# Two decoder layers on one core: the mask of layer 1's context attention added by half-row products

## The chip, the cores and the metric

The kernel runs on one core of one Trainium2 chip. A core has a matrix engine (TensorE, PE in the profile, with its weight loads shown apart as PEld), a vector engine (VectorE, DVE), an activation engine (ScalarE, ACT), a general engine (GpSimd, POOL) and a synchronisation engine (SyncE, SP), which here does nothing but issue transfers (DMAs). Each engine takes its instructions in program order. The metric is the device time of one execution in microseconds (us), the median of several runs.

## The reference

Two post-norm decoder layers work on x of shape 32 x 128 x 128 (batch, tokens, width) with a context of the same shape. In order: a recurrent mix (RWKV), a block with self attention, attention to the context and a feed-forward part (16 heads of 64), a mixture of 8 experts, then in layer 1 a self attention with rotary positions (16 heads of 8), the attention to the context that is changed here, and a mixture of experts with a capacity. A layer norm of the sum follows each. The part that is changed:

```
def _L1_xattn_ref(query, key, value, mask, Wq, bq, Wk, bk, Wv, bv, Wo):
    HEADS = 16
    HEAD_DIM = 8
    SCALE = HEAD_DIM ** (-0.5)
    NEG_INF = -1000000000.0
    ...
    scores = jnp.einsum('bhqd,bhkd->bhqk', q, k) * SCALE
    scores = jnp.where(mask == 0, NEG_INF, scores)
    attn = jax.nn.silu(scores)
    out = jnp.einsum('bhqk,bhkd->bhqd', attn, v)
    out = out.transpose(0, 2, 1, 3).reshape(B, Sq, HIDDEN)
    return out @ Wo.T
...
x = _layernorm(x + _L1_xattn_ref(x, ctx_1024, ctx_1024, mask_Bx1xSxS2_ik1, ...), axis=-1)
```

The mask is an integer array of 32 x 1 x 128 x 128 and is the same for all heads. The attention has a SiLU in place of a softmax, so no maximum and no sum over the row is needed.

## The kernel before

**Tiling.** The batch of 32 is cut into 8 groups of 4 (`G = 4`, so 512 columns a group). Each layer part turns a group into 8 units, and each unit into steps with a lag counted in units (the tables `L5` to `L8`). `build` places all steps of all parts on one time axis, sorts them and writes them out in that order, so that groups and parts follow one another in a software pipeline. A scheduler then orders each engine's instructions; within what data and buffers allow it can move them against the order in which they were written. Buffers come from pools with a tag and a number of buffers (`TAG`, `BUFS`, for PSUM `BANK`, `BANKS`) that are handed out in turn, so that a new use of a buffer waits for the last reader of its old content.

**Layer 1's attention to the context** is `xat_units`. For a group:

- `load` brings x and the context; `pre` transposes x (`xT_ps`, L228) and splits both into a rounded part and its remainder (`split`, L147 and L148).
- `one` projects to queries and keys with three products (`mm3`, L154 to L156) and ACT adds a bias (L1081).
- `part` cuts queries and keys into three bf16 parts on POOL (`parts3`, L783 to L786), and `spill` writes these to DRAM (L807, L809, L810).
- `take` reads them back as a stack (`stack`, L821): head by head, 64 rows for each parity of the head, with the parts of q and k arranged so that one product of 64 rows gives an exact score. Layer 1's self attention goes the same way.
- `mload` loads the group's mask as integers (L1066, tile `mi`, tag `xb`, 2 buffers) and `mask` turns it on DVE into 0 or -1e9 in bf16 (L1070, tile `m`, tag `msk`, 2 buffers).
- `probs(j)`, eight units a group, each with one batch entry and eight heads: two products of the identity with the mask (L1104) start two PSUM banks of 512 columns, one for each parity, the mask being read four times over by a stride of zero. Then eight products of 64 rows and 128 columns (L166, from `block`) add the scores of four heads to each bank. ACT takes the tanh (L1116) and DVE combines it to the SiLU (L1117).
- `values(j)` multiplies with the values in array tiles of 24 columns (L166, `PV<-e`), ACT copies (L853), `oproj` projects (L1130) and adds the residual (L1136), and a layer norm follows (L238, L240, L254). The result is stored (L223) and loaded by the next part (L214).

The order on PE: `block` ties its products to one another in the order in which they are given, and to the block before. The mask products L1104 are issued outside of `block`, so the scheduler can put them apart from the eight products that follow them. Products of three shapes meet in this stage: 128 rows by 128 columns of the array (printed `128*128`), half rows (`64*128`) and the values' `128*24`.

The order on SP: nearly all transfers of the stage go through its queue: x, context, mask, spill and stack of this part and of the self attention before it, and the loads of the expert layer after it. An issue that has to wait for a buffer or for data holds all issues behind it.

Of the kernel before, what the change touches and what calls it, by code (L numbers as in the profile page):

```python
# [11 lines left out]
BF = mybir.dt.bfloat16  # L12
U8 = mybir.dt.uint8
I32 = mybir.dt.int32
AF = mybir.ActivationFunctionType
ALU = mybir.AluOpType
# [6 lines left out]
G = 4  # L23
# [26 lines left out]
L6 = dict(pre=0, rope=2, v=3, part=5, spill=12, take=16, smax=19, mrow=19, mread=4, probs=29, values=30,  # L50
          norm=32, oproj=34, done=38)
L7 = dict(pre=1, one=2, v=3, part=4, spill=9, mask=13, take=13, probs=14, values=16, oproj=18, ln=22, done=24)
L8 = dict(pre=3, logit=4, route=8, load=7, start=11)
FC = dict(load=-11, pre=-10, fc1=-8, fc2=-7, post=-6, done=-5)

# [5 lines left out]
class Later:  # L61


    def __init__(self, get):
        self.get = get
# [5 lines left out]
class Net:  # L71
    def __init__(self, ctx, tc, a, ngroups):
        self.ctx, self.tc, self.nc, self.a, self.ng = ctx, tc, tc.nc, a, ngroups
        nc = self.nc
        self.cst = ctx.enter_context(tc.tile_pool(name="cst", bufs=1))
        self.wp = ctx.enter_context(tc.tile_pool(name="wp", bufs=1))
        self.ps = ctx.enter_context(tc.tile_pool(name="ps", bufs=1, space=PSUM))
        self.sm = ctx.enter_context(tc.tile_pool(name="sm", bufs=3))
        self.dp = ctx.enter_context(tc.tile_pool(name="dp", bufs=1, space=bass.MemoryType.DRAM))
        self.hand = {}  # L80
        self.toturn, self.topv = [], []
        self.last = self.seen = self.pvz = self.dst = self.spare = self.spare2 = None
        self.wk = ctx.enter_context(tc.tile_pool(name="wk", bufs=1))
        self.ident = self.cst.tile([128, 128], F32, name="ident")
        make_identity(nc, self.ident)
        self.identb = self.cst.tile([128, 128], BF, name="identb")
        nc.gpsimd.tensor_copy(self.identb, self.ident)
        self.mhalf = self.cst.tile([128, G], F32, name="mhalf")
        nc.gpsimd.memset(self.mhalf, -0.5)
        self.rev = self.cst.tile([128, 8], F32, name="rev")  # L90
        nc.gpsimd.iota(self.rev, [[-1, 8]], base=8, channel_multiplier=0,
                       allow_small_or_imprecise_dtypes=True)
# [961 lines left out]
    def xat_units(self, g, getw, done):  # L1054
        nc = self.nc
        w = Later(getw)
        st = {}
        b3 = lambda t: t.rearrange("p (b s) -> p b s", s=128)

        def load():  # L1060
            st["x"] = self.getx(g)
            st["c"] = self.ctx_load(g)

        def mload():
            st["mi"] = self.t("mi", [G, 128], I32)
            nc.sync.dma_start(out=st["mi"], in_=self.a["mask1"][:, g * G:(g + 1) * G, :])  # L1066

        def mask():
            st["m"] = self.t("m", [G, 128], BF)
            nc.vector.tensor_scalar(st["m"], st.pop("mi"), 0.0, -1e9, ALU.is_equal, ALU.mult)  # L1070

        def pre():
            st["xh"], st["xl"] = self.split(self.xT_ps(st.pop("x")), "cx")
            st["kh"], st["kl"] = self.split(st.pop("c"), "cc")

        def one(i, xh, xl):
            f = slice(i * 128, i * 128 + 128)
            qp = self.pst("one")
            self.mm3(qp, w["w"][0][:, f], w["w"][1][:, f], xh, xl)
            t1 = self.t("xt")  # L1080
            nc.scalar.activation(t1, qp, AF.Identity, bias=w["b"][:, i:i + 1])  # L1081
            st["t", i] = t1

        def part(i):
            if i == 0:
                st["p"] = self.parts()
            self.parts3(st.pop(("t", i)), [st["p"][:, a, i, :] for a in range(3)], self.t("xr"), i == 1)

        def spill():
            st["d"] = self.spill(g + self.ng, st.pop("p"))  # L1090

        def take(h):
            st["s", h] = self.stack(st["d"], h)

        def vproj(b):
            st["v", b] = self.v9proj(g + self.ng, b, st["kh"], st["kl"], w["w"][0][:, 256:384], w["w"][1][:, 256:384],
                                     w["bv"])

        def probs(j):
            b, pq = j // 2, j % 2  # L1100
            t = slice(b % 2 * 128, b % 2 * 128 + 128)
            s = [self.pst("silu1" if j % 2 else "silu0") for _ in range(2)]
            for par in range(2):
                nc.tensor.matmul(out=s[par], lhsT=self.identb,  # L1104
                                 rhs=st["m"][:, b, :].unsqueeze(1).to_broadcast([128, 4, 128]), start=True, stop=False)
            calls = []
            for k in range(4):
                for par in range(2):
                    r = slice(par * 64, par * 64 + 64)
                    calls.append((s[par][:, k * 128:(k + 1) * 128], st["s", b // 2][r, pq * 4 + k, 1, t],  # L1110
                                  st["s", b // 2][r, pq * 4 + k, 0, t], dict(start=False, stop=k == 3)))
            self.block(calls)
            ps = []
            for par in range(2):
                p = self.t("xp")
                nc.scalar.activation(p, s[par], AF.Tanh, scale=0.5 * 8 ** -0.5)  # L1116
                st["last", j] = nc.vector.scalar_tensor_tensor(p, p, 1.0, s[par], ALU.add, ALU.mult)  # L1117
                ps.append(p)
            st["p", j] = ps

        def values(j):
            st["ob", j // 2] = self.values9(j, st["v", j // 2], st.pop(("p", j)), st.get(("ob", j // 2)),
                                              st.pop(("last", j)))

        def oproj(b):
            ob = st.pop(("ob", b))
            if b == 0:
                st["op"] = self.pst("xout").rearrange("p (b d) -> p b d", d=128)
            for s in range(4):
                nc.tensor.matmul(out=st["op"][:, b, :], lhsT=ob[:, s * 128:(s + 1) * 128],  # L1130
                                 rhs=w["wo"][:, s * 128:(s + 1) * 128], start=s == 0, stop=s == 3)
            if b == G - 2:
                st["x"] = self.getx(g)
            if b == G - 1:
                res = self.tok("xres")
                nc.vector.tensor_tensor(res, st["op"], st["x"], ALU.add)  # L1136
                st["ln"] = self.ln(res, 1e-5)

        units = []
        for j in range(8):  # L1140
            u = [(L7["probs"], lambda j=j: probs(j), 2), (L7["values"], lambda j=j: values(j), 1)]
            if j == 0:
                u += [(0, load), (L7["pre"], pre), (L7["spill"], spill), (L7["mask"] - 2, mload), (L7["mask"], mask)]
                u += [(L7["v"] + b, lambda b=b: vproj(b)) for b in range(G)]
                for i in range(2):
                    u += [(L7["one"] + 2 * i, lambda i=i: one(i, *((st["kh"], st["kl"]) if i else (st["xh"], st["xl"])))),
                          (L7["part"] + 2 * i, lambda i=i: part(i))]
            if j % 4 == 0:
                u.append((L7["take"], lambda h=j // 4: take(h)))
            if j % 2:  # L1150
                u.append((L7["oproj"], lambda b=j // 2: oproj(b)))
            if j == 7:
                u += [(L7["ln"], lambda: st.update(y=st["ln"]())), (L7["done"], lambda: done(st["y"]))]
            units.append([p if len(p) > 2 else (*p, -p[0]) for p in u])
        return units
# [341 lines left out]
def prep(i):  # L1497
    c = np.ascontiguousarray
    f = np.float32
    pairs = lambda w: c(w.reshape(8, 128, 128).transpose(1, 0, 2).reshape(128, 1024))  # L1500
    d = {
        "xtok": c(i["x"].transpose(1, 0, 2)),
        "xT": c(i["x"].transpose(2, 0, 1).reshape(128, 4096)),
        "ctxT": c(i["ctx_1024"].transpose(2, 0, 1).reshape(128, 4096)),
        "mask0": c(i["mask_BxS2_bk0"].reshape(4096)),
        "rwkv_w": c(np.concatenate([i["L0_attn_" + n].T for n in ("Wk", "Wv", "Wr", "Wo")], axis=1)),
        "rwkv_v": c(np.stack([i["L0_attn_" + n] for n in
                              ("mix_k", "mix_v", "mix_r", "spatial_decay", "spatial_first")], axis=1)),
    }
# [23 lines left out]
    b = [i["L1_attn_bq"], i["L1_attn_bk"]]  # L1533
# [17 lines left out]
    wo = np.zeros((4, 4, 32, 128), f)  # L1551
    wo[:, :, :8] = i["L1_xattn_Wo"].T[rows].reshape(4, 4, 8, 128)
    d["x1_wo"] = c(wo.reshape(4, 128, 128).transpose(1, 0, 2).reshape(128, 512))
    d["mask1"] = c(i["mask_Bx1xSxS2_ik1"][:, 0].transpose(2, 0, 1))
    d["m1_gate"] = c(i["L1_ffn_gate_w"].T)
    w1, w3, w2 = (i["L1_ffn_" + n] for n in ("w1", "w3", "w2"))

# [23 lines left out]
```

## Time and profile before

| what | value |
|---|---|
| median of 3 runs | 1859.68 us (1859.35 to 1861.64) |
| the profiled execution, own time | 1864.75 us |
| its span | 1863.0 us, 47015 instructions |
| TensorE clock granted, mean | 0.969 |
| PE busy | 1673.1 us, 90% of the span |
| weight loads | 1360.9 us, 73% |
| DVE busy | 1387.5 us, 74% |
| ACT busy | 1183.3 us, 64% |
| POOL busy | 865.5 us, 46% |
| chain that ended last, by engine | PE 56%, DVE 18%, ACT 9%, DMA 6%, POOL 5%, issue 4% |
| mask products L1104 | 128, from 1382.3 to 1612.9 us |
| mask operations L1070 | 8, from 1192.7 to 1546.9 us |
| mask loads L1066 | 8 of 256 KB, from 1189.9 to 1498.2 us |

How to read it: the page describes one execution. A row of a timeline gives start, duration, engine, line, operation, what it writes and reads (`out<-in`), and the shape; `x8` means that eight such instructions that followed one another are put together. PE's instructions are pipelined, so that durations of neighbours overlap and the distance between starts says more about their cost. "PEclk" is the share of full speed that the clock of TensorE was granted. `SPq` is the time in which SP issues a transfer. In a view of waits, "A <- B" means that A stood idle until B was done. Numbers of buffers are left out of the names.

### The profile page before, as it was taken

The page shows a single profiled execution, that of the slowest core. Times are in us where ns is not written, and L with a number is a line of the kernel's source. Part 1 is how long each engine was busy: PE and PEld are TensorE (multiplying, and loading weights), DVE is VectorE, ACT ScalarE, POOL GpSimd, SP SyncE. Part 2 cuts the span into 40 slices and gives each one's busy share as a digit, 9 for nine tenths or more (in the row PEclk, how much of TensorE's full clock was granted, in tenths as well). Part 3 has the DMA queues.
Part 4 walks back from the last instruction along what each step waited for, and adds up shares of the span by engine and source line. Part 5 has one row for each costly group of instructions (what it writes and reads, how often), then busy time and mean ns, then how long its engine had stood idle before and what let it go on. Part 6 is the DMA issues. An engine that isn't in the chain of part 4 may idle for free.

```text
span 1863.0 us, 47015 instructions
## 1 busy us (share of the span) xinstructions
PE 1673.1 (90%) x16682; PEld 1360.9 (73%) x16682; DVE 1387.5 (74%) x5384; ACT 1183.3 (64%) x3833; POOL 865.5 (46%) x1201
## 2 busy tenths in 40 slices
PE   4898889989999999999899999989779888898898
PEld 3677667767778788887788888866556555688898
DVE  7878988877777777776675767777655767689896
ACT  2775767768777777787645454346567555556664
POOL 4545555564454444453334444336333422246455
PEclk7999999999999999999999999999889989899999
DMA  5101011110110000100134435479878987222222
GB/s 159 36 32 37 26 37 39 34 53 26 48 48 26 26 14 20 48 13 16 62 107 145 159 121 129 111 184 203 192 204 214 226 198 190 74 80 94 94 90 70
DMA packets 148779, 171.58 MB, mean 92 GB/s; under 512 B 13128, under 2 KB 100176, under 8 KB 146064
## 3 DMA queue, kind: packets, MB, share of 16 engines
q1 hardware_dynamic: 145808, 154.95, 31.2%
q0 software_dynamic: 1584, 11.54, 1.5%
q8 instruction: 131, 2.15, 0.5%
q10 hardware_dynamic: 1152, 2.10, 0.3%
q14 instruction: 104, 0.85, 0.2%
HBM read 114.81 MB, written 55.31 MB: 91 GB/s over the span
## 4 chain that ended last, share of the span: by engine, by line
PE 56%; DVE 18%; ACT 9%; DMA 6%; POOL 5%; issue 4%; SPq 1%; ACTq 0%; POOLq 0%; DVEq 0%
PE PV L166 7%; PE mm L154 6%; PE mm L532 6%; PE S L749 6%; PE S L166 5%; PE mm L155 5%; PE mm L156 5%; ACT e L474 5%; DMA x<-x 3%; DVE e L469 3%; PE PT L1327 3%; PE PT L165 2%; DVE x L254 1%; POOL e L478 1%; PE S L598 1%
## 5 line engine op out<-in xcount | busy, mean ns | idle before, releaser
L474 ACT ACTIVATE e<-e,nm 128x128 f32<-128x128 f32 x1024 | 397.5, 390 | 95.6 <-POOL nm L471 95.5
L478 POOL TENSOR_TENSOR e<-e,ri 128x512 f32<-128x512 f32 x256 | 267.3, 1048 | 258.8 <-DVE ri L476 192.8
L469 DVE CUSTOM_DVE_ANT_0 e<-S,msk 128x128 f32<-128x128 f32 x1024 | 225.2, 282 | 11.9 <-PE S L166 11.7
L474 ACT ACTIVATION_READ_ACCUMULATOR e<-e,nm 128x1 f32 x1024 | 192.3, 188 | 0.0
L166 PEld LDWEIGHTS S<-qk 64*128 64x128 f32 x2048 | 126.0, 189 | 72.0 <-issue 41.2
L166 PE MATMUL S<-qk 64*128 64x128 f32 x2048 | 150.1, 286 | 29.6 <-DVE pt L492 20.6
L154 PE MATMUL mm<-xs,w 128*128 128x512 f32 x296 | 130.6, 444 | 35.0 <-ACT xs L147 11.5
L166 PE MATMUL PV<-pt,v 128*64 128x128 f32 x2048 | 141.7, 281 | 3.5 <-DVE big L516 2.5
L476 DVE RECIPROCAL ri<-su 128x4 f32<-128x4 f32 x256 | 43.8, 172 | 135.4 <-ACT e L474 134.8
L738 ACT ACTIVATE v<-mm,col_moe_b 128x512 f32<-128x512 f32 x128 | 85.1, 684 | 79.4 <-PE mm L156 78.9
L749 PEld LDWEIGHTS S<-w,v 128*128 128x128 f32 x1024 | 128.6, 191 | 7.8
L749 PE MATMUL S<-w,v 128*128 128x128 f32 x1024 | 133.7, 276 | 0.0
L492 ACT COPY pt<-PT 128x256 f32<-128x256 f32 x256 | 81.6, 371 | 68.6 <-PE PT L165 68.2
L532 PE MATMUL mm<-w,big 128*128 128x128 f32 x1024 | 122.1, 277 | 0.0
L532 PEld LDWEIGHTS mm<-w,big 128*128 128x128 f32 x1024 | 117.5, 192 | 4.9 <-issue 2.9
L155 PE MATMUL mm<-xs,w 128*128 128x512 f32 x296 | 118.6, 401 | 1.6 <-DVE xs L148 1.6
L166 PEld LDWEIGHTS PV<-pt,v 128*64 128x64 f32 x2048 | 110.6, 138 | 12.7 <-DVE big L516 2.9
L156 PE MATMUL mm<-xs,w 128*128 128x512 f32 x296 | 117.8, 398 | 0.0
L166 PE MATMUL PV<-e,w 128*24 128x128 f32 x2048 | 88.1, 292 | 26.5 <-ACT e L974 11.3
L267 POOL TENSOR_SCALAR rsqv<-bmv 128x4 f32<-128x4 f32 (+1 forms) x73 | 14.4, 197 | 202.1 <-DVE bmv L240 185.5
L853 ACT COPY v<-PV 128x256 f32<-128x256 f32 x128 | 47.9, 374 | 92.3 <-PE PV L166 91.8
L154 PEld LDWEIGHTS mm<-xs,w 128*128 128x128 f32 x296 | 55.5, 189 | 61.5 <-ACT xs L147 16.2
(306 smaller groups left out, 4782.2 us busy)
## 6 DMA issues: line engine op xcount, KB each, us to landing
x<-x SPq DMA_DIRECT2D x151, 256.0 KB
big<-d_st SPq DMA_DIRECT2D x52, 512.0 KB
pt<-d_w SPq DMA_DIRECT2D x64, 256.0 KB
d_st<-qk SPq DMA_DIRECT2D x48, 256.0 KB
d_st<-qk SPq DMA_DIRECT2D x16, 768.0 KB
d_w<-big POOLq DMA_DIRECT2D x11, 1024.0 KB, 5.2
w<-d_w SPq DMA_DIRECT2D x7, 1024.0 KB
w<-d_st SPq DMA_DIRECT2D x12, 512.0 KB
```

The lines of the kernel that those rows point to most:

```text
L154: mm(out=out, lhsT=wh, rhs=xh, start=True, stop=False)
L155: mm(out=out, lhsT=wh, rhs=xl, start=False, stop=False)
L156: mm(out=out, lhsT=wl, rhs=xh, start=False, stop=True)
L166: return self.nc.tensor.matmul(out=out, lhsT=lhsT, rhs=rhs, **more)
L469: self.seen = nc.vector.tensor_tensor_reduce(e[:, t], s[h][:, t], msk[:, t], 1.0, NEG, ALU.add, ALU.max, mx[:, b:b + 1])
L474: nc.scalar.activation(e[:, t], e[:, t], AF.Exp, bias=nm[:, b:b + 1], scale=0.125, accum_out=su[:, b:b + 1])
L478: i = nc.gpsimd.tensor_tensor(e3, e3, ri.unsqueeze(2).to_broadcast([128, G, 128]), ALU.mult)
L492: last = (nc.vector.tensor_copy if h else nc.scalar.copy)(d, s_)
L532: nc.tensor.matmul(out=o[:, b, :], lhsT=st["ot", p // 4][:, p % 4, b * 128:(b + 1) * 128], rhs=w["wo"][:, p * 128:(p + 1) * 128], start=p ...
L738: nc.scalar.activation(h, hp, AF.Gelu, bias=w["b1"][:, k:k + 1])
L749: nc.tensor.matmul(out=o[:, b, :], lhsT=hs[i][:, b * 128:(b + 1) * 128], rhs=w["w2"][:, k * 128:k * 128 + 128], start=i == 0, stop=i == 1)
L1327: nc.tensor.matmul(out=o[:, 0:N], lhsT=a_, rhs=b_, start=n == 0, stop=n == len(prods) - 1)
```

## The change

The mask is loaded, converted and multiplied in another arrangement.

- On the host, `mask1` of (128 queries, 32 entries, 128 keys) becomes (128, 32, 2, 128): the 128 queries are cut into two halves, and partition p holds, for both halves, the row p mod 64. So each of the two halves of the partitions has the whole mask.
- A group's mask is therefore twice as large. It is loaded and converted in two steps of two batch entries (`mload(h)`, `mask(h)`), the second one `MSTEP = 2` units after the first.
- A second matrix beside the identity, `rollb`, has the identity's column halves exchanged. It is made once by two copies on POOL.
- In `probs`, the two products of 128 rows become four of 64 rows: for each half z of the queries and each parity a product of 64 rows of `identb` or `rollb` with the mask's half, over the same 512 columns. The two parities use different halves of the array's rows and different PSUM banks. They are the first four calls of the unit's `block`, ahead of its eight products.

```
+MSTEP = 2
...
+        self.rollb = self.cst.tile([128, 128], BF, name="rollb")
+        nc.gpsimd.tensor_copy(self.rollb[:, 0:64], self.ident[:, 64:128])
+        nc.gpsimd.tensor_copy(self.rollb[:, 64:128], self.ident[:, 0:64])
...
-        def mload():
-            st["mi"] = self.t("mi", [G, 128], I32)
-            nc.sync.dma_start(out=st["mi"], in_=self.a["mask1"][:, g * G:(g + 1) * G, :])
-
-        def mask():
-            st["m"] = self.t("m", [G, 128], BF)
-            nc.vector.tensor_scalar(st["m"], st.pop("mi"), 0.0, -1e9, ALU.is_equal, ALU.mult)
+        def mload(h):
+            st["mi", h] = self.t("mi", [2, 2, 128], I32)
+            nc.sync.dma_start(out=st["mi", h], in_=self.a["mask1"][:, g * G + h * 2:g * G + h * 2 + 2])
+
+        def mask(h):
+            if h == 0:
+                st["m"] = self.t("m", [G, 2, 128], BF)
+            nc.vector.tensor_scalar(st["m"][:, h * 2:h * 2 + 2], st.pop(("mi", h)), 0.0, -1e9, ALU.is_equal, ALU.mult)
...
             s = [self.pst("silu1" if j % 2 else "silu0") for _ in range(2)]
-            for par in range(2):
-                nc.tensor.matmul(out=s[par], lhsT=self.identb,
-                                 rhs=st["m"][:, b, :].unsqueeze(1).to_broadcast([128, 4, 128]), start=True, stop=False)
             calls = []
+            for z in range(2):
+                for par in range(2):
+                    r = slice(par * 64, par * 64 + 64)
+                    calls.append((s[par], (self.rollb if z ^ par else self.identb)[r],
+                                  st["m"][r, b, z, :].unsqueeze(1).to_broadcast([64, 4, 128]),
+                                  dict(start=z == 0, stop=False)))
...
-                u += [(0, load), (L7["pre"], pre), (L7["spill"], spill), (L7["mask"] - 2, mload), (L7["mask"], mask)]
+                u += [(0, load), (L7["pre"], pre), (L7["spill"], spill), *((L7["mask"] - 2 + MSTEP * h, lambda h=h: mload(h)) for h in range(2)),
+                      *((L7["mask"] + MSTEP * h, lambda h=h: mask(h)) for h in range(2))]
...
-    d["mask1"] = c(i["mask_Bx1xSxS2_ik1"][:, 0].transpose(2, 0, 1))
+    m = i["mask_Bx1xSxS2_ik1"][:, 0].transpose(2, 0, 1).reshape(2, 64, 32, 128).transpose(1, 2, 0, 3)
+    d["mask1"] = c(np.concatenate([m, m]))
```

In the compiled program PE has 256 mask products where it had 128, each with its own weight load; DVE has 8 operations more, SP 8 transfers more and POOL 2 copies more. Outside of these every engine has the same instructions, in a partly different order from about 1190 us on.

## The prediction

> **What bounds the kernel now.** I read the page's time slices, then the busy time by stretch around the changed lines, then those lines' own rows, then the queues they stand in.
>
> ```profile
> PE   4898889989999999999899999989779888898898
> PEclk7999999999999999999999999999889989899999
> DMA  5101011110110000100134435479878987222222
> ```
>
> TensorE (PE) is at eight tenths or more nearly everywhere, so PE is the bound of the whole. The exception is slices 29 to 35 (1304 to 1630 us), where PE falls to 7 and 8 and its clock to 8, while the DMA engines stand at 7 to 9 until 1584. The changed lines run there. By stretch (PE, weight loads, DVE, ACT, POOL busy; then clock, DMA share, GB/s):
>
> ```profile
> 1382.00:1400.00 18.00, 9.24 (x95) 4.63 (x94) 2.64 (x8) 6.90 (x15) 4.05 (x5) 0.62 1.05 239
> 1400.00:1470.00 70.00, 63.87 (x873) 42.39 (x872) 49.40 (x116) 47.98 (x103) 30.75 (x41) 1.00 0.93 220
> 1470.00:1526.00 56.00, 45.09 (x532) 29.55 (x536) 34.03 (x72) 27.65 (x57) 16.73 (x20) 0.85 0.85 211
> 1526.00:1573.00 47.00, 45.81 (x638) 29.71 (x638) 36.13 (x76) 31.29 (x68) 12.17 (x14) 1.00 0.94 214
> 1573.00:1622.00 49.00, 37.30 (x295) 27.34 (x295) 30.95 (x89) 22.94 (x59) 9.07 (x10) 0.79 0.16 51
> ```
>
> Two stretches (70 and 47 us) have PE 91% and 97% busy at full clock: less PE work shortens them. The others hold PE gaps and a lowered clock: what ends the gaps sets them. The waits of PE between 1180 and 1615 us name it (total, times, longest):
>
> ```profile
> PE PT L228 <- DMA x<-x: 12.9, 4, 5.9
> ```
>
> These are the transposes of x of a later group; three of the four lie at 1472, 1494 and 1520 us. The x load stands in SP's queue behind the stacks (L821, 2 MB a group), and these behind the landing of the spill (L807):
>
> ```profile
> 1496.04 0.37 SPq L809 DMA_DIRECT2D d_st<-qk  x1
> 1498.16 0.34 SPq L1066 DMA_DIRECT2D xb<-in_mask_dram  x1
> 1498.60 0.39 SPq L807 DMA_DIRECT2D d_st<-qk  x1
> ...
> 1504.43 5.09 SPq L821 DMA_DIRECT2D big<-d_st  x4
> 1509.57 3.63 SPq L214 DMA_DIRECT2D x<-x  x2
> ```
>
> The mask load L1066 stands in this queue too. Here it waited for the mask operation of an earlier group, which gave its buffer back (DVE, 1497.71 for 0.42), and held L807, whose data POOL had ready at 1497.26.
>
> **The change, part by part.**
>
> *Mask products.* The rows of the removed ones, and a piece of PE's timeline:
>
> ```profile
> L1104 PE MATMUL mm<-msk,identb x64: 376/384/634, 1382.3 to 1602.9; 128*128 128x512 bf16 x64
> L1104 PE MATMUL S<-msk,identb x64: 379/389/650, 1398.9 to 1612.9; 128*128 128x512 bf16 x64
> ```
>
> ```profile
> 1450.64 0.39 PE L1104 MATMUL mm<-msk,identb 128*128 128x512 bf16 x1
> 1450.96 0.40 PE L166 MATMUL mm<-big 64*128 64x128 bf16 x8
> 1451.29 0.39 PE L1104 MATMUL mm<-msk,identb 128*128 128x512 bf16 x1
> 1451.52 0.59 PE L1104 MATMUL S<-msk,identb 128*128 128x512 bf16 x2
> 1452.04 0.64 PE L166 MATMUL PV<-e,w 128*24 128x128 f32 x16
> 1452.61 0.40 PE L166 MATMUL S<-big 64*128 64x128 bf16 x8
> 1452.94 0.71 PE L1130 MATMUL PT<-pt,v 128*128 128x128 f32 x4
> ```
>
> Durations overlap, so I take start to start. A mask product followed by one of the same shape takes 0.23 (1451.29 to 1451.52), or 0.216 as the median of such pairs. Followed by another shape it takes 0.32 (1450.64 to 1450.96). So a change of the array's shape costs about 0.095 us. Eight half-row products of 128 columns take 0.33 with such a change: 0.23 for 1024 columns, as long as one mask product needs for 512. The two halves of the rows therefore run side by side.
>
> The trace has no half-row product of 512 columns. Bounds per unit of four: side by side 2 x 0.216 = 0.43, what the two whole ones cost now; one after the other 0.86, over 64 units +27.6 us. I take the first, since the eight half-row products are the nearest row.
>
> What is saved is shape changes. Counted in the compiled order of PE, the stage has 249 before and 207 after: 42 x 0.095 = 4.0 us of PE work. By share of mask products (87 of 128 in the two PE-bound stretches), 2.7 us lie where PE sets the pace. The second of those stretches ends in a wait for the stored x (4.8 us of PE gap at 1573.8), which takes back part: I count -2, bounds 0 and -4.
>
> The Trainium skill (TensorEngine Tiling (Array Packing), section Instruction Overhead) speaks against the change: about 60 cycles of overhead for every matmul, and there are 128 more. At the 2.4 GHz that the skill's TensorE: Matmul & The Clock Gate states, that is 25 ns each, an estimate of +3.2 us. The eight products above show no such addition beyond their columns, so my sum goes without it; with it, it would be +3.2 us.
>
> *Place on PE.* The mask products are now tied to their unit's block; before, they stood where a gap was expected. So less PE work stands ahead of the transposes that wait for x. Summing start-to-start prices along both orders, the first transpose stands 1.86 us (the fourth only 0.43), 0.91 and 0.91 us of work earlier at 1472, 1494 and 1520. PE then arrives earlier at a wait whose end does not move, and does that work afterwards. With 1.1 for the first this is +2.9 us; bounds 2.2 and 3.7. At 1573.8, where two or three mask products filled in ahead of the gap, 0.4 to 0.65 more. Against this the three groups each save 5 changes of shape after their wait, 0.5 each: -1.5. Together +2, bounds 0 and +3.5.
>
> *Mask operation.* 16 instead of 8 of L1070 on DVE, each of 418 ns at least, 428 in the median, 1314 at most: +3.4 to +10.5 us of DVE, +5.6 by the mean of 0.70. DVE is 61 to 77% busy from 1400 to 1573, and two of the additional ones run before 1250 under PE's full load. Of the other six the chain of waits passes through one such operation of eight (1546.88, 1.31 us): +0.5, bounds 0 and +2.6. If DVE's slack were gone, +3.4.
>
> *Mask loads.* 16 instead of 8, of 256 KB each. At the 182 to 289 GB/s of 20-us stretches there, one takes 0.9 to 1.4 us. In the compiled order six stand early and ten in the crowded stage, where there were four. Three pairs now stand after L807 and before the stack; L807 is no longer held by a mask load (-1.3 at 1498.6, -0.3 at 1470.8). The pairs run in the 5 to 6 us in which SP waits for the spill's landing; if that cover were gone, 2 x 0.9 to 1.4 a group. One pair stands ahead of L807, at 1448. Net +0.5 us, bounds -2 and +6.
>
> *Setup.* Two POOL copies of 128 x 64 at the start: POOL's largest 512-element rows take 1.3 us, so under 1.3 each, beside the first loads (PE idles 10 us there). Nothing; +2.6 without that cover.
>
> *Sum.* -2 + 2 + 0.5 + 0.5 = +1 us. The profiled execution took 1864.75 (span 1863.0 and 1.75 around it), 5.07 above the median of the runs. So 1865.75 there, and 1859.68 + 1 = 1860.7, rounded to **1861**.
>
> **The rivals.**
>
> *PE sets the pace (faster).* If the waits for x move with PE, because the same chain feeds the next spill, all 4.0 us count, and L807's earlier issue shortens the loads as well (-1.6). A wait shortened below what lowers the clock gives more. The rows: the gap of 1.2 us at 1494 left the clock at 1.00, that of 4.6 us at 1472 went with 6.8 us at half rate, a loss of 3.4. That makes -5.6 to -9; I take **1853**. For it: 63.87 of 70 and 45.81 of 47 us busy. Against it: PE's longest waits end with DMA, and more work now stands behind them.
>
> The Trainium skill (TensorE: Matmul & The Clock Gate, section What's actually happening) puts the threshold at an idle window of about 3.4 us; by it, the gap of 1.2 us could grow by 2 without loss, whereas by rows alone that growth costs 0 to 3.4.
>
> *SP's queue holds the stacks (slower).* One mechanism: the pair of mask loads before a stack waits for the previous group's mask operations, and these stand on DVE behind work that itself waits for PE. At the stack issued at 1525.16 there was no mask load; now its pair waits for two operations behind L872 (1525.13), two L1117 (0.6 each) and themselves (0.84): 1527.2, then two issues of 0.35, so the stack starts at 1527.9 or later, +2.7. At 1477.22 the masks stand behind L148, which ended at 1474.6: free by 1475.5 to 1477.2, and 1.8 to 2.8 us of bytes go ahead of the stack. Queued behind are the stacks, then the x loads that PE waits for. It decides once the spill lands before the mask operations are done. Two such holds of 2.7, and one more clock window of 3.4, make +8.8 less the 2 gained: **1867**.
>
> *Half rows do not overlap.* Then +27.6 us, less 4.0: 1883. Against it stand the eight products in 0.33. I give it 3 in 100.
>
> **How the numbers follow.** The balance near zero 0.41, PE's pace 0.30, SP's hold 0.26, no overlap 0.03. The likeliest is 1861, its own range 1857 to 1865. A measurement tells 0.2% (3.7 us) from no change: below 1855.96 or above 1863.40. The balance lies inside three times in four (0.31), below 0.03, above 0.07. So faster 0.33, same 0.31, slower 0.36. The range runs from 1850 (PE's pace down to about -9) to 1872 (holds with one clock window more), leaving out the far end of both rivals and the lack of overlap.
>
> **What would show it.** Half-row mask products starting in pairs, 0.43 us for four; PE's busy time some 4 us lower; waits of the transposes (12.9 us in all) longer by about 3; L807 following POOL at once; stacks starting within 6 us of L807. I am wrong if four mask products take 0.86; if the stacks at 1477 and 1525 start late and x lands later; or if the waits for x shrink with PE's work. The order after the stage changes on every engine too, in the same instructions, and could add a few us either way that no row here prices.

## The result and the profile after

| | before | after |
|---|---|---|
| median, same chip | 1860.1 us (1859.35 to 1861.64, 4 runs) | 1879.0 us (1877.48 to 1880.76, 4 runs) |
| ratio, 95% interval | | 1.0096 (1.0079 to 1.0112) |
| profiled execution, its span | 1864.75, 1863.0 | 1877.48, 1875.7 |
| mean clock granted | 0.969 | 0.965 |
| PE busy | 1673.1 us | 1677.8 us |

The change makes the kernel 18.9 us slower. The forecast was 1861 us, with a range from 1850 to 1872; it was wrong. The two profiled executions lie only 12.7 us apart in span: that of before is 4.65 us above its median, that of after 1.5 below.

The time slices of after, to be laid beside those of before:

```profile
PE   4898989889899999998899999989779788889998
PEclk7999999999999999999999999999899889999999
DMA  5101111010110000001134434678979978222222
```

PE and its clock sag in the same part, only longer. The busy time by stretch (PE, weight loads, DVE, ACT, POOL; clock; DMA share, GB/s):

```profile
1402.00:1462.00 60.00, 55.55 (x813) 38.55 (x803) 40.64 (x102) 42.52 (x91) 24.51 (x34) 1.00 0.89 228
1462.00:1602.00 140.00, 111.77 (x1431) 73.92 (x1425) 90.13 (x203) 70.87 (x146) 36.22 (x43) 0.84 0.79 186
```

Before, the full-clock stretches from 1400 to 1470 and from 1526 to 1573 had PE 91% and 97% busy. Now there is no second one: from 1462 to 1602 us PE is busy 80% of the time, at a mean clock of 0.84. PE's waits between 1180 and 1615 us (total, times, longest):

```profile
PE PV L171 <- DVE e L1127: 15.4, 7, 4.7
...
PE PT L233 <- DMA x<-x: 9.3, 4, 5.5
PE mm L159 <- DVE pt L911: 8.0, 2, 4.6
```

The wait for the stored x (L228 before, 12.9 us) has not grown. New are waits of the values' products for the SiLU on DVE (4.8 us in one wait before) and one of 4.6 us before the stage has begun. The mask products themselves behave as forecast, as a piece of PE's timeline shows:

```profile
1442.56 0.39 PE L171 MATMUL S<-msk,identb 64*128 64x512 bf16 x1
1442.56 0.60 PE L171 MATMUL S<-msk,rollb 64*128 64x512 bf16 x2
1442.79 0.38 PE L171 MATMUL S<-msk,identb 64*128 64x512 bf16 x1
1443.00 0.39 PE L171 MATMUL S<-big 64*128 64x128 bf16 x8
```

A pair begins at the same instant and the next pair 0.23 us later; the four take 0.44 us until the scores begin. The rival that they do not overlap falls.

**Where the time is lost.** ACT has the same 3833 instructions in all these kernels. I paired them by their source line and their rank in it, and took the median difference of their starts from those of before, by stretches of 40 us of the time before (us; one execution each; the kernels e1 to e21 are those of the next section):

```
at        1160   1200   1240   1400   1440   1480   1520   1600   end
after     -1.5   +4.0   +3.3   +1.0   +2.4  +11.4  +12.7   +9.9  +12.7
e6        -2.0   +3.0   +3.7   +1.7   +2.5   +2.6   +1.0   +4.9   +6.2
e12       -2.2   -2.2   -2.9   -0.3   +2.2   +9.4  +11.7   +9.4   +9.5
e15       -2.9   +2.6   +4.2   +2.6   +7.5  +12.3  +12.6  +11.3  +13.9
e16       -2.4   -2.4   -3.5   -5.3   -3.4   -0.7   +0.3   -2.8   -0.2
e18       -1.7   -1.6   -0.7   -1.7   -0.3  +12.0  +13.0  +13.3  +13.4
e19       +0.3   +0.3   +1.9   -1.7   +0.2   +4.6   +3.6   -0.9   +1.2
e20       +1.9   +7.4   +7.2   +5.9  +10.7  +14.4  +13.5  +13.5  +15.8
```

The changed kernel loses 5.5 us at about 1220 us, in the self attention ahead of the stage, and gets part of it back. It then loses 9 to 10 us between 1440 and 1520.

The first loss, in DVE's timeline and then in PE's:

```profile
1227.95 0.43 DVE L1077 TENSOR_SCALAR msk<-xb 128x512 bf16<-128x512 int32 x1 [5.37 <-DMA xb<-in_mask_dram]
1228.30 0.74 DVE L911 SCALAR_TENSOR_TENSOR pt<-mm,col_a_b,w 128x512 f32<-128x512 f32 x1
```

```profile
1229.10 0.47 PE L159 MATMUL mm<-w,cs 128*128 128x128 f32 x1 [4.58 <-DVE pt L911]
```

A convert of the second group's mask stands in DVE's queue before its load has landed. DVE waits 5.37 us, the instruction behind it is what PE needs, and PE waits 4.58 us; 6.8 us at half clock go with it. The load is late: with two loads a group in two buffers it is the fourth, issued at 1220.22 behind a stack, where before the second load, at 1193.12, brought the second group's whole mask.

For the second loss the orders of three queues are suspects. On SP the mask pair now stands between spill and stack:

```profile
1474.17 0.36 SPq L812 DMA_DIRECT2D d_st<-qk  x1
1483.49 0.82 SPq L1072 DMA_DIRECT2D xb<-in_mask_dram  x2
1484.49 5.61 SPq L826 DMA_DIRECT2D big<-d_st  x4
```

The stack follows the spill by 10.3 us; before it was 6.4 us (1470.79 to 1477.22). On PE, in two groups the four transposes of the next x have moved ahead of the group's second projection. Before:

```profile
1491.69 0.50 PE L154 MATMUL mm<-v,w 128*128 128x512 f32 x1
...
1494.30 0.66 PE L228 MATMUL PT<-ident,x 128*128 128x128 f32 x4 [1.22 <-DMA x<-x]
```

After, on PE and then on POOL:

```profile
1502.29 1.11 PE L233 MATMUL PT<-ident,x 128*128 128x128 f32 x4 [1.79 <-DMA x<-x]
1503.05 0.78 PE L159 MATMUL mm<-v,w 128*128 128x512 f32 x1
```

```profile
1505.49 0.62 POOL L788 TENSOR_SCALAR qk<-pt 128x512 bf16<-128x512 f32 x1 [7.61 <-ACT pt L1088]
```

The projection does not read x, but it now waits for x behind the transposes. POOL, which cuts its result into parts, stands idle for 7.61 us, and the spill comes at 1509.33, where it came at 1498.60. The spill is followed by the stacks, these by the load of a later x: the delay goes round and meets PE again at the next transposes. On DVE, finally, the layer norm's last step (L259, 3.2 us for its four operations) now stands ahead of a pair of SiLU operations (L1127) that a unit of values waits for, 2.3 to 2.6 us in four places.

What ends the hold of the mask pair on SP (9.0 us, 1474.53 to 1483.49) is a convert of the group before, which stands on DVE behind work on the late x:

```profile
1482.23 0.68 DVE L153 TENSOR_TENSOR xs<-PT,xs 128x512 fp32r<-128x512 f32 x1
1483.04 0.76 DVE L1077 TENSOR_SCALAR msk<-xb 128x512 bf16<-128x512 int32 x2
```

Much of the second loss is then paid in clock. The stretches at half clock between 1400 and 1575 us, before (two) and after (four; the last, 1552.40 to 1555.80, is shown further below):

```profile
1471.72:1478.55 6.83, 6.43 (x56) 4.83 (x56) 2.17 (x4) 2.04 (x4) 0.00 (x0) 0.50 0.64 241
1516.09:1526.33 10.24, 5.69 (x45) 2.98 (x49) 1.89 (x4) 2.04 (x4) 2.64 (x3) 0.50 0.78 244
```

```profile
1467.10:1484.16 17.06, 11.55 (x83) 7.35 (x78) 4.49 (x11) 4.90 (x10) 3.54 (x4) 0.50 0.73 196
1501.23:1508.06 6.83, 5.78 (x35) 3.64 (x36) 1.47 (x3) 1.65 (x3) 2.39 (x3) 0.50 0.15 52
1525.12:1535.36 10.24, 9.26 (x69) 5.72 (x70) 3.43 (x7) 3.11 (x6) 2.61 (x4) 0.50 0.46 134
```

PE was busy in them for 12.1 us before and for 30.0 us after. Four mask products that take 0.44 us at full clock take 0.83 in them (at 1481.96), so the 17.9 us more are worth some 9 us, an estimate.

### The profile page after: what moved, and what is told of

Same layout as the page of the kernel before. It is cut to its first block, busy times and chain, and to the rows that moved or that the text cites. A ratio compares the mean times of both kernels' runs of the same rounds, so it can differ in the third digit from the quotient of the medians.

```text
span 1875.7 us, 47303 instructions
## 1 busy us (share of the span) xinstructions
PE 1677.8 (89%) x16810; PEld 1368.1 (73%) x16810; DVE 1392.5 (74%) x5392; ACT 1186.8 (63%) x3833; POOL 865.2 (46%) x1203
## 4 chain that ended last, share of the span: by engine, by line
PE 55%; DVE 17%; ACT 9%; DMA 6%; POOL 6%; issue 5%; SPq 2%; POOLq 0%; ACTq 0%; DVEq 0%
PE mm L537 6%; PE PV L171 6%; PE mm L159 6%; PE S L754 6%; PE S L171 5%; PE mm L160 5%; PE mm L161 5%; ACT e L479 5%; DMA x<-x 3%; DVE e L474 3%; PE PT L1338 2%; PE PT L170 2%; POOL e L483 2%; PE mm L171 1%; PE S L603 1%
## 5 line engine op out<-in xcount | busy, mean ns | idle before, releaser
L474 DVE CUSTOM_DVE_ANT_0 e<-S,msk 128x128 f32<-128x128 f32 x1024 | 225.3, 283 | 12.0 <-PE S L171 11.8
L171 PE MATMUL PV<-e,w 128*24 128x128 f32 x2048 | 88.2, 294 | 38.5 <-DVE e L1127 15.4
L272 POOL TENSOR_SCALAR rsqv<-bmv 128x4 f32<-128x4 f32 (+1 forms) x73 | 14.5, 198 | 229.9 <-DVE bmv L245 213.9
```

The costliest lines, as they stand in the source:

```text
L171: return self.nc.tensor.matmul(out=out, lhsT=lhsT, rhs=rhs, **more)
L474: self.seen = nc.vector.tensor_tensor_reduce(e[:, t], s[h][:, t], msk[:, t], 1.0, NEG, ALU.add, ALU.max, mx[:, b:b + 1])
```

## The experiments

Ratios are to the kernel before on the same chip. "Order" always means a dependency without a semaphore between two instructions of one engine.

| run | what is different | median us | before | ratio (95%) |
|---|---|---|---|---|
| e1 | after, layer norm step later | 1882.42 | 1859.93 | 1.0108 (1.0088 to 1.0128) |
| e2 | before, layer norm step earlier | 1870.39 | 1859.93 | 1.0049 (1.0034 to 1.0064) |
| e4 | before, whole rows in the block | 1860.1 | 1859.93 | 0.9995 (0.9982 to 1.0009) |
| e6 | before, mask loaded and converted twice | 1873.3 | 1859.93 | 1.0061 (1.0038 to 1.0084) |
| e1b | as e1, one more SiLU later | 1879.35 | 1859.7 | 1.0103 (1.0085 to 1.0122) |
| e7 | after, second load in another tag | 1904.59 | 1859.7 | 1.0237 (1.0215 to 1.0259) |
| e8 | e7 and e1b | 1900.46 | 1859.7 | 1.0218 (1.0197 to 1.0238) |
| e9 | e6, second load in another tag | 1879.3 | 1859.7 | 1.0112 (1.0088 to 1.0136) |
| e10 | e7 with a third tag | 1889.55 | 1862.92 | 1.0135 (1.0112 to 1.0158) |
| e12 | after, one load, doubled by copies | 1873.69 | 1862.92 | 1.0054 (1.0036 to 1.0072) |
| e13 | before, more bytes | 1874.34 | 1862.92 | 1.0057 (1.0041 to 1.0073) |
| e14 | before, a wait on the mask load | 1868.85 | 1862.92 | 1.0026 (1.0013 to 1.0038) |
| e15 | after, projection first | 1874.09 | 1861.21 | 1.0068 (1.0050 to 1.0086) |
| e16 | e12, projection first | 1867.72 | 1861.21 | 1.0033 (1.0019 to 1.0046) |
| e18 | before, transposes first | 1875.74 | 1861.21 | 1.0079 (1.0057 to 1.0101) |
| e19 | e16 and e1b's order | 1871.47 | 1865.72 | 1.0029 (1.0015 to 1.0042) |
| e20 | e15 and e1b's order | 1879.6 | 1865.72 | 1.0073 (1.0054 to 1.0093) |
| e21 | e12, products outside the block | 1872.2 | 1865.72 | 1.0039 (1.0026 to 1.0051) |

**e1 and e1b, e2: the order on DVE.** My first theory was the new wait for the SiLU.

```
+                self.silus.append(st["last", j])
...
+                    self.tc.add_manual_dep(i.ins, after.ins.name, mybir.DependencyInfo(
+                        mybir.DependencyClass.NoSync, mybir.DependencyReason.DATA), reason="order")
```

> The changed kernel, with one order added on DVE: the four LN applies of a group may not stand ahead of the fourth product of tanh that follows the group's residual (a dependency without a semaphore, so no new wait). In the order on DVE, 4 or 5 such products then stand between residual and applies, as before the change; in the changed kernel it was 3 in four of the groups 1 to 5. Theory O (the order on DVE): the four waits of PV for the product of tanh of 2.6 us each and the half-rate windows behind them go, the run comes to 1860 to 1868 us. Theory D (the doubled mask: twice the bytes, twice the converts, twice the loads on SP's queue): those are all still there, 1874 to 1881. Theory H (the four half-row products in the block, or that they are tied to its place): still there too, 1874 to 1881.

> The changed kernel with the LN applies held one product of tanh longer than in the first run of this kind: 5 or 6 such products stand ahead of them instead of 4 or 5, so that the applies no longer come between the two products of a pair, which is what the trace of the first run showed (its waits of PV were still 2.0 to 2.4 us each, so that run had not undone the order). Theory O (order on DVE): the waits of PV for the product of tanh in the groups 1 to 5 go, and what is left is the cost of the doubled mask, 11 us in the run that doubled it alone: 1866 to 1874 us. Theory Q (SP's queue held by the second mask load) alone: 1875 to 1882. Theory H (half rows in the block): 1875 to 1882.

Neither brought anything back. In e1 the waits were still there, with up to 2.4 us each. In e1b they were gone (2.0 us in two waits from 1420 to 1640 us), but PE waited 16.6 us for x in that stretch instead, in three waits of up to 9.4. PE only waited for another reason, and the time of the stage stayed as it was.

In e2 it is the other way round: in the groups 1, 3, 4 and 5 the layer norm step is written four units earlier (a lag of 18 in place of 22), and the next SiLU written after it has to follow it.

> The kernel before, with the opposite order forced on DVE in the groups 1, 4 and 5: the LN applies stand ahead of the fourth product of tanh (3 of them between residual and applies, as in the changed kernel). No mask or product is touched. Theory O: three waits of PV of 2.6 us each appear, with half-rate windows behind some of them: 1866 to 1876 us. Theories D and H: nothing that they price has changed, 1858 to 1863.

It is 0.49% slower, as theory O has it, but it is not clean: in its compiled order three transposes also moved ahead of the projection in one group. By itself it would have misled me.

**e4: the tie to the block.**

```
-                nc.tensor.matmul(out=s[par], lhsT=self.identb,
-                                 rhs=st["m"][:, b, :].unsqueeze(1).to_broadcast([128, 4, 128]), start=True, stop=False)
...
+                calls.append((s[par], self.identb, st["m"][:, b, :].unsqueeze(1).to_broadcast([128, 4, 128]),
+                              dict(start=True, stop=False)))
```

> The kernel before, with its two whole-row mask products moved into the block of the unit's products, and nothing else: the mask is loaded and converted once, no half rows. In DVE's order 4 or 5 products of tanh stand between residual and applies, so the wait that theory O prices cannot come back. Theory O: 1856 to 1864 us. Theory D: 1856 to 1864. Theory H, if the tie to the block is what costs: 1870 to 1880; if the half rows are, 1856 to 1864.

No difference: the tie alone costs nothing. In its compiled order the projection stays ahead of the transposes.

**e6: the doubled mask alone.**

```
+                                 rhs=st["m"][:, b, 0, :].unsqueeze(1).to_broadcast([128, 4, 128]), start=True, stop=False)
...
+    d["mask1"] = c(np.stack([m, m], 2))
```

> The mask handling of the changed kernel alone: two loads of 2 KB a row for each group and two converts, as in the changed kernel, but the mask held there twice in whole rows, and the two whole-row products of the kernel before, issued where it issued them, ahead of the block. DVE's order has 4 or 5 products of tanh between residual and applies. Theory O: only the small terms remain, 1860 to 1866 us. Theory D: most of the 19 us, 1870 to 1880, with SP holding the stacks behind a mask load. Theory H: 1859 to 1863.

It costs 0.61%, more than half of the whole, with no half row and none of the moved orders on PE or DVE. Its loss at 1200 us is the same 5.0 us.

**e7, e8, e9, e10: another buffer for the second load.** The tile `mi` has two buffers, so a group's two loads need both, and each waits for a convert of the group before. With another tag for the second one this wait should go.

```
-            st["mi", h] = self.t("mi", [2, 2, 128], I32)
+            st["mi", h] = self.t("mi2" if h else "mi", [2, 2, 128], I32)
```

> The changed kernel, but its second mask load goes into a buffer of another tag, with five buffers of which the stage uses one a group, so that it need not wait for the converts of the group before; the scheduler then issues it behind the stacks. DVE's order is the one of the changed kernel (3 products of tanh between residual and applies, in all of the groups 1 to 5). Theory Q: SP's queue no longer waits for the mask converts, about the 11 us of the run that doubled the mask alone are saved: 1865 to 1871 us, with the waits of PV of 2.6 us still in the trace. Theory O alone: 1875 to 1882. Theory H: 1875 to 1882.

> The changed kernel with both: the second mask load in a buffer of the other tag, and the LN applies behind 5 products of tanh. The half-row products stay in the block as the change has them. Theories O and Q together: 1855 to 1864 us, level with the kernel before or a little better, for the shape changes saved. Only one of them: 1866 to 1874. Theory H: 1872 to 1882.

> The run that doubled the mask alone (whole-row products as in the kernel before), with the second load in a buffer of the other tag. DVE's order is that of the kernel before, 4 products between residual and applies. Theory Q (the doubled mask costs by its hold on SP's queue): 1858 to 1865 us. If it costs by its bytes and its converts on DVE: 1868 to 1875, as in the run without the other tag.

> The changed kernel with the second mask load in another tag's buffers, this time one that leaves both loads ahead of the stacks in SP's order (with the tag used before, the second load stood behind the stacks, its data came up to 11 us late, and DVE stood still for it: 1904.6 us, which said nothing of the hold). The bytes, the converts, the half rows and the order of the LN applies on DVE (3 products ahead of them) are the changed kernel's. Theory Q (SP's queue is held because the two buffers hold only one group's mask, so that each load waits for the converts of the group before): 1862 to 1871 us. Theory B (the 256 KB more a group on a DMA ring that is full from the spill until x has landed): 1874 to 1881. Theory H (half rows in the block): 1874 to 1881.

All four are slower than the kernels that they come from, so they give no price for the hold. They do bear on the first loss: in the measure of the table above each of them loses 0.0 us between 1160 and 1200, where e6 loses 5.0, and e9 differs from e6 by the tag alone. In e7 the scheduler put the second load behind the stacks, and DVE waited for it (1420 to 1640 us):

```profile
DVE msk L1077 <- DMA cs<-in_mask_dram: 47.4, 6, 11.0
```

In e10, where both loads stand ahead of the stacks, the projection stands behind the transposes in three groups instead of two, and a mask load held SP for up to 11.8 us.

**e12: half rows without the second load.** The mask is loaded and converted once, and two copies move each half to the other partitions.

```
+            nc.vector.tensor_scalar(st["m"][:, 0], mi, 0.0, -1e9, ALU.is_equal, ALU.mult)
+            for z in range(2):
+                nc.vector.tensor_copy(st["m"][z * 64:z * 64 + 64, 1], st["m"][64 - z * 64:128 - z * 64, 0])
```

> The changed kernel without its second load: the mask is loaded and converted once in whole rows, as before the change, and two copies on DVE move each half to the other 64 partitions. The half-row products and their place in the block stay, and so does the order of the LN applies (3 products ahead of them). Theories Q and B: the cost of the load is gone, 1858 to 1868 us. Theory H: 1874 to 1881. Theory O (the order of the applies), which the two runs that moved the applies did not bear out: 1868 to 1880, with the waits of PV of 2.6 us.

0.42% comes back, with intervals apart from the changed kernel's. Half of the loss is the second load, the other half is not. In the table by stretches the 5 us at 1220 are gone and the loss from 1440 to 1520 is still there.

**e13 and e14: how the load costs.**

```
+            more = self.dp.tile([128, G, 128], I32, name=f"more_{g}")
+            nc.sync.dma_start(out=more, in_=self.a["mask1"][:, g * G:(g + 1) * G, :])
```

> The kernel before, with each group's mask moved once more behind its load, from DRAM to another place in DRAM that nobody reads: 256 KB more a group on the same queue, and no wait, no buffer, no convert and no change in the order on any other engine. Theory B: 1868 to 1874 us, the cost of the run that doubled the mask alone. Theory Q: 1860 to 1864.

The time fits theory B and the trace refutes it: as nothing waits for these copies, all eight were issued between 35 and 42 us. They moved their 2 MB there (0.12 and 35 GB/s before in this stretch):

```profile
40.00:60.00 20.00, 16.26 (x111) 11.93 (x109) 17.12 (x73) 10.50 (x43) 7.97 (x16) 0.91 0.45 136
```

By 80 us this run was 7.0 us late, so what the bytes cost in the stage stays open.

```
+                self.tc.add_manual_dep(i.ins, self.conv.ins.name, mybir.DependencyInfo(
+                    mybir.DependencyClass.Sync, mybir.DependencyReason.DATA), reason="hold")
```

> The kernel before, with one wait added and nothing else: each mask load waits on SP for the convert of the group before, as the second load of the changed kernel does for want of a buffer. No byte and no convert more; the order on DVE, PE and ACT is that of the kernel before. Theory Q: 1866 to 1876 us. Theory B: 1858 to 1862.

The hold alone costs 0.26%. One place shows it, on SP:

```profile
1518.75 0.38 SPq L810 DMA_DIRECT2D d_st<-qk  x1
1527.17 0.35 SPq L1067 DMA_DIRECT2D xb<-in_mask_dram  x1
1527.61 0.39 SPq L808 DMA_DIRECT2D d_st<-qk  x1
```

The mask load waits there for a convert (8.0 us is the longest such wait), and the last part of the spill stands behind it.

**e15, e16, e18: the order on PE.** The transposes may not stand ahead of the group's second projection.

```
+            if after is not None:
+                self.tc.add_manual_dep(i.ins, after.ins.name, mybir.DependencyInfo(
+                    mybir.DependencyClass.NoSync, mybir.DependencyReason.DATA), reason="order")
...
+            st["xh"], st["xl"] = self.split(self.xT_ps(st.pop("x"), self.ones.get(g - 1)), "cx")
...
+            self.ones[g] = self.mm3(qp, w["w"]
```

> The changed kernel with one order restored on PE, by a dependency without a semaphore: the four transposes of a group's x may not stand ahead of the second projection of the group before. In the changed kernel they did in two groups, and the projection waited there for x from DMA, and with it POOL's parts, the spill, the stacks and the next x. Half rows, doubled mask and both mask loads stay; the LN applies stand behind 5 products of tanh in the groups 2 to 4 and behind 3 in the groups 1 and 5. Theory P (PE's order of projection and transposes): 1864 to 1872 us, the cost of the doubled mask alone, 11 us, being all that is left. If the half rows or their place in the block cost by themselves (theory H): 1874 to 1881.

> The same order restored on PE in the kernel that loads the mask once and doubles it by two copies on DVE (1873.7 us against 1862.9 in its own comparison). Half-row products in the block, no second load, projection ahead of the transposes. Theory P: nothing that costs is left, a ratio of 0.996 to 1.002 to the kernel before. Theory H: still 1.004 to 1.007.

> The converse: the kernel before, whole-row products and single mask as they were, with the four transposes of the next group's x forced ahead of the second projection on PE in the groups 3 to 5, as the changed kernel has it in two groups and the one with the copies in three. SP's order is that of the kernel before. Theory P: 1868 to 1876 us, the transposes waiting for x and the spill 4 to 7 us later in each of these groups. Theory H: 1858 to 1863.

With the order restored, the changed kernel gains 0.28% and e12 gains 0.21%. Each of these differences is about as large as its intervals, but both go the same way. In e15's trace the loss between 1400 and 1520 is still 10.0 us, against 11.7 in the changed kernel, and the projection hardly starts earlier in the two groups (1504.75 and 1528.06, against 1503.05 and 1530.06): it now stands behind a unit of values that waits 2.28 us for the SiLU. The converse is larger: in the kernel before, with whole rows and a single mask, this order, forced in three groups, costs 14.5 us. In its trace PE waits longer at the transposes, with the projection behind them:

```profile
1472.50 0.90 PE L231 MATMUL PT<-ident,x 128*128 128x128 f32 x3 [9.56 <-DMA x<-x]
...
1504.04 1.11 PE L231 MATMUL PT<-ident,x 128*128 128x128 f32 x4 [7.65 <-DMA x<-x]
1504.80 0.78 PE L156 MATMUL mm<-v,w 128*128 128x512 f32 x1
```

It loses 12 us between the columns 1440 and 1480 of the table. But the three groups forced are 3 to 5, counted from 0 (projections at 1445, 1474 and 1504 us); the changed kernel has the exchange in 5 and 6 (1503 and 1530), e12 in 4 to 6. So e18 shows what such an exchange can cost, and not what the two of the changed kernel cost.

**e19, e20, e21: what is left.**

> Half-row products in the block, the mask loaded once and doubled by two copies on DVE, the projection ahead of the transposes on PE, and the LN applies behind 5 or 6 products of tanh, so that they stand between two pairs: all three causes undone, the half rows and their place kept. If the rest of e16 is the order of the applies (theory O): a ratio of 0.996 to 1.001 to the kernel before. If it is the half rows or their place (theory H): 1.002 to 1.005, as in e16 (1.0033).

> The changed kernel with both orders restored, on PE and on DVE, and its two mask loads kept. Theories D and Q together (the doubled mask by bytes and by its hold on SP): 1.004 to 1.007, what the load cost alone in the kernel before (1.0061). If the load costs nothing once the orders are right: 0.998 to 1.002.

Restoring DVE's order as well gives 0.04% in e19 against e16 and -0.05% in e20 against e15: nothing. In e20's trace other waits stand in the place of those for the SiLU: SP is held by a mask load that waits for a convert (9.9 us, 1480.4 to 1490.3), and PE waits 6.7 us for x. e20 against e19 prices the second load once more, at 0.44%. And 0.29% is left in e19.

> Half rows and the mask doubled by copies, but the four mask products are issued free, ahead of the block, where the kernel before issued its two; so the block begins with the products of queries and keys as before. The scheduler is left to order the rest: 4 or 5 products of tanh ahead of the applies, the projection ahead of the transposes. Theories P and O: 0.996 to 1.002, both orders being right without a dependency written by hand. Theory H, by the half rows themselves: 1.002 to 1.006.

The interval fits theory H, and the trace shows its reason. Issued free, the products are in most units ordered bank by bank, and then both of a bank lie in the same half of the rows:

```profile
1496.17 0.39 PE L1115 MATMUL mm<-msk,identb 64*128 64x512 bf16 x1
1496.40 0.38 PE L1115 MATMUL mm<-msk,rollb 64*128 64x512 bf16 x1
```

They follow one another by 0.23 us; four in such an order would take 0.92, an estimate, instead of 0.44. PE was busy 1693.3 us, 22.4 more than in e19 (1670.9). A part of that goes to changes of shape around the scattered products: between the first and the last mask product the trace of e21 has 285 of them, that of e19 213. So half rows need an order that keeps the pairs together, as the block gives it, and e21 does not bear on what e19 has left.

## Why the prediction was wrong

*Mask loads and mask operation.* This is the larger error. The two terms were +0.5 us each. Measured with and without the second load they are 0.42% (after against e12), 0.35% (e15 against e16) and 0.44% (e20 against e19): 6.5 to 8.2 us. The step that failed is the sentence that "two of the additional ones run before 1250 under PE's full load" and so cost nothing, and that of the loads "six stand early". I priced DVE's slack and not the queue: an operation that waits for its load holds all of DVE behind it. All six kernels whose doubled mask shares the two buffers of `mi` (after, e1, e1b, e6, e15, e20) lose 5.0 to 5.5 us there between 1160 and 1200 in the table's measure. None of e12, e16, e19 and e21, which have one load, does, and none of e7 to e10, whose second load has its own buffer. The changed kernel gets 3.0 us of this back by 1400, so a part of the 6.5 to 8.2 us lies elsewhere. That it is the hold of SP is argued: the hold forced by itself (e14) costs 0.26%, and the bytes were not isolated.

*Place on PE.* It was +2 us, bounds 0 and +3.5. I counted work that moves behind the transposes as fill that is done later, against "a wait whose end does not move". But the projection is part of that work, and it feeds POOL's parts, the spill, the stacks and so a later x: the end does move. Measured 0.28% and 0.21%, 4 to 5 us with an uncertainty nearly as large, and 14.5 us in e18, in three groups of which one is the changed kernel's. The compiled order showed the exchange; I had added up the durations in it and not asked who waits for each. The sign that I gave for this term did not come: the waits of the transposes, foretold 3 us longer, fell from 12.9 to 9.3 us.

*What has no term.* The waits for the SiLU behind the moved layer norm step grew from 4.8 to 15.4 us, and the work at half clock grew by an estimated 9 us. The sum has neither; a longer time at half clock stands only in a rival, as one window worth 3.4 us. The waits for the SiLU alone do not make the loss: e1b and e20 are nearly without them (2.0 us from 1420 to 1640, 3.1 from 1400 to 1640) and no faster than the changed kernel and e15. Projection, spill, convert, mask load, stack and x form a loop, and the traces show another wait in it where one is taken away.

*SP's queue holds the stacks.* This rival named the stacks of 1477 and 1525 at 2.7 us each. The first came, with 3.9 us more between spill and stack; in the group of 1525 the stack follows the spill by 3.9 us (1536.34 to 1540.21). The mechanism was right, its place half right, and its total too small without the other two.

*Shape changes.* The -2 us is not seen: PE is busy 4.7 us longer, at a slightly lower clock. No run isolates it. With it falls the rival that PE sets the pace, which counted 4.0 us of it.

*Products side by side*: right, 0.44 us for four against 0.43 foretold.

*The sum.* The steps from after to e12, e16 and e19 are 0.42% for the second load, 0.21% for PE's order and 0.04% for DVE's, which leave 0.29% (5 us, interval 0.15 to 0.42). What that rest is stays open: e19 still differs from before by the half rows, by two copies on DVE a group (0.59 us together) and by exchanges on every engine. One of these is not small and was not tested by itself: though e19 has a single mask load a group, SP stands 9.9 us behind the one issued at 1479.94, which waits for a convert; before, its like was issued at 1470.33, 0.46 us ahead of the last part of the spill. The tie alone is excluded by e4. A version with half rows and no doubled mask at all was not tried: in it both halves of the rows would write each bank, and would have to take the two banks in turn. The Trainium skill (TensorEngine Tiling (Array Packing), section Gotcha 1: PSUM Pressure) says that different row tiles cannot use a bank at the same time; no run here shows it. No version beat the kernel before.

## What to carry to other kernels

Where a stage is a loop (load, transpose, project, cut, spill, load again), a moved instruction is priced by what waits for its result and not by its duration; compare each engine's compiled order, and ask at every exchange whether something inside the loop now stands behind a wait that it did not have. A wait that is removed and brings nothing need not have been outside the loop: here another took its place each time (PE's for x, up to 9.4 us, in e1b; SP's for a convert in e20). And a copy or a load that has its slack in bytes may still have none in its queue, so look at what stands behind it there.

## What was not expected of the hardware

PE's clock fell after gaps shorter than I had assumed. In the changed kernel, clock and PE at one of the waits for the SiLU:

```profile
1549.60:1552.40 2.80, 0.21 (x8) 0.21 (x12) 2.80 (x7) 0.10 (x1) 1.25 (x1) 1.00 1.23 189
1552.40:1555.80 3.40, 3.40 (x33) 2.15 (x26) 1.42 (x3) 0.37 (x1) 0.00 (x0) 0.50 1.07 325
```

A gap of 2.6 us is followed by 3.4 us at half rate. In e16 a gap of 2.3 us at 1488.2 left the clock at 1.00 (1475.9 to 1513.4), while one of the same length that ended at 1512.5 was followed by 13.7 us at half rate, so the length alone does not decide. The Trainium skill (TensorE: Matmul & The Clock Gate, section What's actually happening) gives an idle window of about 3.4 us; the lengths at half rate here are near multiples of that (3.4, 6.8, 10.2, 13.7 us), but a gap of 2.6 was enough.
